# Seven block products for the second product of both feed-forward blocks, all joins on ScalarE, sums and scores in PSUM, byte masks, three transposition buffers and a new written order

## The chip, the core and the metric

One NeuronCore of a Trainium2 chip runs the whole program. The engines are TensorE (PE, matrix products into PSUM; its weight loads are listed as PEld), VectorE (DVE), ScalarE (ACT), GpSimd (POOL) and SyncE (SP), whose queue issues nearly all DMA transfers. All data are float32. The time is the device time of one launch in microseconds (us); the kernel before took 3119.91, 3129.46 and 3135.92 us in three runs, so the median is 3129.46 us.

## What is computed

64 independent graphs of 256 nodes with 256 features go through two layers. Cut to what matters:

```python
# layer 0
h = gat(x, adj, W1, a1); h = gat(h, adj, W2, a2)      # e = leaky_relu(Wh1 + Wh2^T), masked where adj <= 0,
h = layernorm(x + h, g_ln1, b_ln1)                    # softmax over axis 1, att @ Wh
x = layernorm(h + relu(h @ w_ff1 + b_ff1) @ w_ff2 + b_ff2, g_ln2, b_ln2)
# layer 1, 8 heads of width 32
p = softmax(q @ k^T / sqrt(32))
out = sum over r of (p * (adj == r)) @ v_r            # r = 0..3
x = layernorm(x + out @ Wo + bo, g1, beta1)
x = layernorm(x + gelu(x @ W1 + b1) @ W2 + b2, g2, beta2)
```

The inputs hold only 0 and 1 in `adj`, which the fast path (`binary`) uses: `v_0` is applied to all of `p`, and `v_1 - v_0` to `p * adj`. A slow path (`general`) stands behind a test of the maxima of `adj` and is not entered with these inputs.

## The kernel before

**Stages.** A graph passes through many small pieces of work, each a Python closure under a name. The letter is the stage: `L` loads, `G` the two attention steps of layer 0 and norm A, `F` the first feed-forward block with norm B and the projections, `A` the eight attention heads, `T` the output projection, norm C, the second feed-forward block, norm D and the store. `S` pieces prepare weights once. Nodes and features are both cut into two halves of 128, so a 256x256 matrix is 2x2 blocks.

**Order.** The order of all instructions on PE, DVE, ACT, POOL and SP is written out by hand in three lists (L43 to L158) and kept as written: `START`, then `PERIOD` once for each of 59 periods, then `END`. An entry such as `T.fa/5` means piece `T.fa` of the graph five behind the newest. So six graphs are in flight at once, and one graph is finished in each period. Every engine works its own share of the list in order; an instruction whose input is late holds all behind it on its engine.

**Seven products.** `seven_products` (L597) multiplies two matrices of 2x2 blocks with seven block products and sums of blocks instead of eight. Its pieces are `a` to `e` (the products, into three PSUM banks X, Y, Z), `k1` to `k4` (a first result taken out of a bank) and `p1` to `p3` (a bank added to a result, L637). It serves the first product of both feed-forward blocks (`h`, PE L661), the values of the heads (`v`, PE L848) and the second product of the block in `T` only (`f`, PE L702, with its sums `T.u0` to `T.u3` on POOL at L584 into the tile `H`). The second product of the block in `F` is plain: `F.f0` and `F.f1` (L682 to L689), 8 products each of 128x128 by 128x256 into the bank `ff_a`. Each float32 product shows as two instructions in the trace.

**Turning by DMA.** `turned` (L461) transposes a tile in three steps: `dt` (SP L469) a transposing DMA into `pairs`, `dm` (SP L477) two copies by DMA into `halves`, and a join (L484), a copy that interleaves 16-bit halves. `pairs` and `halves` have two tiles each. The joins of the eight heads are `A.mg00` to `A.mg13`, where the first digit is the group of four heads; head 0 of both groups is joined on POOL, the other six on ACT. The joins into columns (`F.cA`, `F.cB`, `T.cC`) are on ACT.

**Norms.** `layernorm` (L493): `ln` adds the residual on DVE (L502) into the SBUF tile `acc` and takes the moments (L507 to L510), `rs` takes the root on POOL (L514), `nm` writes the normed rows on DVE (L519).

**Scores of layer 0.** For steps A and B: `G.e` puts target scores in a PSUM bank (L763), `G.lr` adds source scores on ACT into the SBUF tile `s` (L771), `G.ad` does the leaky ReLU (L776), the mask (L777, with the byte tile `away`) and the maximum (L779) on DVE in place, `G.ex` the exponential on ACT (L784), `G.rz` scales the rows on DVE (L794), and `G.gA0`, `G.gA1`, `G.gB` are products (L800).

**Masks of the heads.** `A.pm` (L922) multiplies a joined head by the int32 tile `adj` on DVE. `adj` has four tiles, since a graph's adjacency lives from its load to its last head.

Of the kernel before, what the change touches and what calls it, by code (L numbers as in the profile page):

```python
# [25 lines left out]
F32 = mybir.dt.float32  # L26
U8 = mybir.dt.uint8
# [7 lines left out]
P = 128  # L35
# [8 lines left out]
G.nmA/1 A.mx13/3 A.rz12/3 F.raB/4 F.sB/3 T.hk3/5 A.mx11/3 A.rz10/3 L.xT/0 T.hp3/5 A.vp2/4 A.dm02/4  # L44
A.pm03/4 G.wh0/0 A.mg02/4 T.hd/5 A.ex13/3 T.hp2/5 G.wh1/0 A.ex11/3 A.sp12/3 A.dm00/4 G.wc0/0
A.sp10/3 G.wc1/0 A.ve/4 A.pm01/4 F.dtA/1 A.mg00/4 F.dmA/1 F.f1/2 A.pm02/4 G.eA/0 A.pm00/4 T.rbC/5
F.rbB/4 A.vk4/4 T.he/5 T.ge0/5 A.rz11/3 A.pm11/4 A.rz13/3 A.dt10/3 F.lnB/2 A.sc0/3 A.o0/4 T.ge1/5
A.mx00/3 G.lrA/0 F.cA/1 T.hk4/5 A.o1/4 T.ge2/5 A.sp11/3 A.sp13/3 A.mx02/3 A.dt12/3 F.ha/1 A.oc0/4
T.ge3/5 L.adj/0 A.oc1/4 F.sA/1 A.ex00/3 F.hb/1 A.mx03/3 G.away/0 A.dm10/3 A.dm12/3 F.rsB/2 F.hk1/1
F.hk2/1 T.wo/4 A.mx01/3 G.adA/0 A.mg10/3 T.u0/5 F.hp1/1 T.lnC/4 F.hc/1 T.u1/5 A.mg12/3 A.dt13/3  # L50
G.exA/0 F.raA/1 A.dt11/3 F.nmB/2 A.ex03/3 A.dm13/3 G.rzA/0 T.fa/5 F.hk3/1 A.ex02/3 T.rsC/4 T.fb/5
F.hd/1 T.nmC/4 G.gA0/0 T.u3/5 T.fk1/5 T.fk2/5 A.rz03/3 A.ex01/3 T.u2/5 F.hp2/1 L.x/0 F.hp3/1
A.mg13/3 A.sp03/3 G.gA1/0 A.pm12/3 G.wd0/0 G.wd1/0 A.dm11/3 A.rz01/3 T.fc/5 A.va/3 A.vb/3 F.dtB/2
T.fk3/5 A.mg11/3 F.rbA/1 A.sp01/3 F.r0/1 A.pm13/3 T.dtC/4 A.rz02/3 A.vk1/3 G.eB/0 T.fd/5 F.dmB/2
T.fp1/5 A.vk2/3 G.lrB/0 T.fp2/5 F.cB/2 F.he/1 A.vc/3 T.dmC/4 T.fe/5 A.rz00/3 F.r1/1 G.adB/0
A.dt03/3 T.cC/4 A.dt01/3 F.q/2 A.vk3/3 G.exB/0 F.hk4/1 A.vp3/3 T.fp3/5 F.qe0/2 F.k/2 A.sp02/3
T.fk4/5 F.r2/1 T.ha/4 F.qe1/2 A.dm03/3 F.ke0/2 T.hk1/4 T.lnD/5 G.rzB/0 T.nmD/5 A.sp00/3 T.sC/4
G.gB/0 A.vp1/3 T.hb/4 A.dm01/3 T.rsD/5 A.dt02/3 T.raC/4 F.ke1/2 T.rbD/5 T.hp1/4 A.sc1/2 T.out/5
A.dt00/3 G.lnA/0 A.mg03/3 T.hk2/4 F.r3/1 A.mg01/3 A.mx12/2 A.mx10/2 A.vd/3 G.rsA/0 T.hc/4 A.pm10/3
F.f0/1 A.ex12/2 A.ex10/2  # L60
# [5 lines left out]
G.away:0 L.adj:2 S.lw:0 S.v0:0 L.adj:1 G.wh0:0 G.wh1:0 G.wc0:0 G.wc1:0 G.eA:0 G.lrA:0 G.adA:0  # L66
S.f0:0 G.exA:0 G.rzA:0 G.gA0:0 G.gA1:0 G.wd0:0 G.wd1:0 S.f1:0 G.eB:0 G.lrB:0 S.f2:0 L.xT:1 G.wh1:1
G.adB:0 G.wh0:1 L.xT:2 G.exB:0 G.rzB:0 G.wc0:1 G.wc1:1 G.gB:0 G.wh0:2 G.eA:1 G.away:1 G.lrA:1
G.lnA:0 G.rsA:0 G.nmA:0 G.adA:1 F.dtA:0 F.raA:0 G.exA:1 S.p2:0 S.v1:0 G.wh1:2 S.q0:0 G.wc0:2
G.rzA:1 G.wc1:2 G.gA0:1 G.gA1:1 L.xT:3 G.eA:2 G.wd0:1 F.dmA:0 S.v2:0 S.q1:0 G.wd1:1 G.eB:1 F.cA:0  # L70
G.lrB:1 F.sA:0 G.adB:1 G.lrA:2 L.x:1 F.ha:0 S.lr:0 F.hk1:0 F.hb:0 G.away:2 G.adA:2 F.hk2:0 F.hc:0
F.hk3:0 F.hp3:0 F.hd:0 F.hp2:0 G.exB:1 F.he:0 F.r0:0 F.hp1:0 G.wh1:3 G.rzB:1 S.j1:0 G.gB:1 G.lnA:1
F.r1:0 F.hk4:0 F.r2:0 F.r3:0 G.wh0:3 F.f0:0 G.wc0:3 G.exA:2 L.adj:3 G.rsA:1 G.nmA:1 G.rzA:2 F.f1:0
G.gA0:2 F.rbA:0 G.gA1:2 F.lnB:0 G.wd0:2 L.x:2 L.xT:4 G.wc1:3 S.v3:0 G.wh1:4 G.wd1:2 F.rsB:0
F.dtA:1 F.dmA:1 G.eA:3 G.eB:2 G.lrB:2 F.cA:1 F.nmB:0 G.wh0:4 G.adB:2 G.lrA:3 F.ha:1 F.sA:1 G.exB:2
F.hb:1 F.dtB:0 F.hk1:1 F.raB:0 G.rzB:2 G.away:3 F.dmB:0 F.hk2:1 G.gB:2 G.lnA:2 G.wc0:4 F.cB:0
F.hc:1 F.k:0 G.adA:3 G.rsA:2 G.wc1:4 G.nmA:2 F.hk3:1 F.ke0:0 F.q:0 F.ke1:0 F.hp3:1 F.hd:1 F.qe0:0
L.x:3 F.hp1:1 F.hp2:1 F.qe1:0 F.r0:1 A.sc1:0 F.raA:1 A.mx13:0 F.he:1 A.mx10:0 F.r1:1 A.ex13:0
F.dtA:2 F.hk4:1 F.rbB:0 F.raA:2 F.r2:1 A.sc0:0 F.r3:1 A.rz13:0 A.mx12:0 A.mx00:0 A.sp13:0 F.dmA:2
G.exA:3 A.ex10:0 A.ex12:0 A.mx01:0 A.ex01:0 A.dt13:0 A.rz10:0 G.rzA:3 A.rz12:0 F.cA:2 F.sB:0  # L80
F.f0:1 F.f1:1 G.gA0:3 A.sp10:0 F.rbA:1 A.dm13:0 A.mx02:0 A.ex02:0 A.mg13:0 A.dt10:0 A.rz01:0
A.ex00:0 G.wd0:3 G.gA1:3 A.sp12:0 F.lnB:1 A.dt12:0 A.va:0 A.vb:0 A.mx11:0 G.wd1:3 A.sp01:0 F.rsB:1
A.vk1:0 G.eB:3 A.dm10:0 A.dm12:0 A.mg10:0 F.nmB:1 G.lrB:3 F.dtB:1 A.ex11:0 A.mg12:0 A.mx03:0
S.l0:0 F.ha:2 F.hk1:2 A.rz00:0 A.dt01:0 G.adB:3 A.pm10:0 A.rz11:0 F.sA:2 A.vk2:0 F.dmB:1 A.rz02:0
F.hb:2 F.hk2:2 A.dm01:0 A.vc:0 F.hc:2 A.ex03:0 S.l1:0 A.vk3:0 A.pm13:0 A.vd:0 F.cB:1 A.sp11:0
A.rz03:0 F.k:1 G.exB:3 A.vp1:0 F.hk3:2 A.mg01:0 A.sp02:0 F.ke0:1 F.hp1:2 G.rzB:3 F.hp3:2 F.q:1
A.dt11:0 F.rbA:2 A.vp2:0 F.ke1:1 F.hd:2 A.ve:0 F.qe0:1 F.qe1:1 A.dt02:0 A.dm11:0 A.sp00:0 F.hp2:2
G.gB:3 A.pm12:0 A.dm02:0 A.vk4:0 A.sp03:0 G.lnA:3 S.l2:0 A.mg11:0 F.he:2 F.r0:2 A.sc1:1 G.rsA:3
A.mx11:1 F.hk4:2 A.mg02:0 A.mx12:1 A.vp3:0 A.ex11:1 A.sc0:1 F.r1:2 A.dt03:0 A.rz11:1 A.mx13:1
# [97 lines left out]
def binary(ctx: ExitStack, tc: tile.TileContext, t, most, out: bass.AP):  # L187
# [1125 lines left out]
```

## Time and profile before

The profiled execution took 3121.47 us, of which its span is 3119.7 us; the median of the three timed runs is 8.0 us above it. The granted clock of TensorE was 0.992 of full speed over the span.

| what | us | share of the span | per graph (by 64) |
|---|---|---|---|
| TensorE busy | 3007.0 | 96% | 47.0 |
| VectorE busy | 2747.0 | 88% | 42.9 |
| ScalarE busy | 2548.7 | 82% | 39.8 |
| GpSimd busy | 2290.2 | 73% | 35.8 |
| DMA engines, mean of 16 | | 68% on SP's queue | |

A busy TensorE is one with a product in its pipeline, so its share says that it is seldom empty, not that it runs at its peak. For the slope one reads the distance from one group of products to the next. VectorE, ScalarE and GpSimd are given as the time in which an instruction ran.

### The profile page before, as it was taken

What the parts mean: (1) busy time and instruction counts of PE and PEld (TensorE: products, weight loads), DVE (VectorE), ACT (ScalarE), POOL (GpSimd) and SP (SyncE); (2) the same over time, 40 slices, a digit from 0 to 9 for tenths busy, and PEclk for the clock granted to TensorE, in tenths of its full rate; (3) what the DMA queues carried; (4) which work ended last, traced back from release to release, by engine and by line L of the source; (5) the groups of instructions that cost most, each with busy time, mean ns of one, the idle gap of its engine ahead of it and who ended that gap; (6) DMA issues with size and microseconds to landing.
All of it is one profiled execution on the core that took longest, in us unless ns stands there. A gap on an engine that the chain in (4) does not pass through costs nothing.

```text
span 3119.7 us, 68789 instructions
## 1 busy us (share of the span) xinstructions
PE 3007.0 (96%) x23270; PEld 2629.7 (84%) x23270; DVE 2747.0 (88%) x5744; ACT 2548.7 (82%) x5822; POOL 2290.2 (73%) x3057
## 2 busy tenths in 40 slices
PE   6899999999999999999999999999999999999986
PEld 5788888888888888888898888888888888888876
DVE  5689999899998899898999899999999999889965
ACT  2688888888888888888888888888888888878874
POOL 4568777777777777777777777777777777777765
PEclk9999999999999999999999999999999999999998
DMA  5577766677676777776676666677677776767663
GB/s 156 108 145 149 149 149 143 146 155 143 149 151 137 142 146 151 148 152 138 155 150 144 148 142 145 150 152 147 147 153 145 149 149 143 146 138 151 149 133 73
DMA packets 1023941, 449.41 MB, mean 144 GB/s; under 512 B 771008, under 2 KB 1021888, under 8 KB 1023584
## 3 DMA queue, kind: packets, MB, share of 16 engines
q1 hardware_dynamic: 1022320, 442.70, 67.9%
q8 instruction: 188, 3.08, 0.5%
q0 software_dynamic: 976, 1.72, 0.4%
q14 instruction: 169, 1.38, 0.2%
q10 hardware_dynamic: 288, 0.52, 0.1%
HBM read 58.87 MB, written 16.78 MB: 24 GB/s over the span
## 4 chain that ended last, share of the span: by engine, by line
PE 68%; DVE 12%; DMA 8%; issue 3%; ACT 3%; POOL 1%; SPq 1%; DVEq 0%; ACTq 0%; POOLq 0%
PE ff_a L686 11%; PE hX_c L661 6%; PE o L930 5%; PE fX_c L702 5%; PE hX_a L661 4%; PE sc L880 3%; PE q L835 3%; PE hY_c L661 3%; PE k L835 3%; PE gat_b L800 3%; PE vX L848 3%; PE wh L747 3%; DVE pm L922 2%; PE wo L949 2%; DMA adj<-in_adjT 2%
## 5 line engine op out<-in xcount | busy, mean ns | idle before, releaser
L484 ACT COPY pm<-halves_p 128x1024 uint16<-128x1024 uint16 x384 | 522.4, 1360 | 137.8 <-DMA halves_p<-pairs_p 135.7
L922 DVE TENSOR_TENSOR pm<-pm,adj 128x512 f32<-128x512 f32 x512 | 565.6, 1123 | 19.3 <-POOL pm L484 12.2
L686 PE MATMUL ff_a<-w_L_gnn_w_ff,hid_a 128*128 128x256 f32 x2048 | 463.0, 379 | 0.1
L686 PEld LDWEIGHTS ff_a<-w_L_gnn_w_ff,hid_a 128*128 128x128 f32 x2048 | 384.0, 190 | 50.4 <-ACT hid_a L678 0.8
L484 POOL COPY pm<-halves_p 128x1024 uint16<-128x1024 uint16 x128 | 180.2, 1408 | 157.5 <-DMA halves_p<-pairs_p 140.4
L930 PE MATMUL o<-pm,v 128*32 128x256 f32 x4096 | 235.3, 381 | 5.5 <-POOL p L907 2.4
L678 ACT ACTIVATE hid_a<-hid_a,col_L_gnn_b_ff 128x256 f32<-128x256 f32 x512 | 230.1, 500 | 3.3 <-DVE hid_a L637 3.2
L678 ACT ACTIVATE hid_c<-hid_c,col_L_gnn_b 128x256 f32<-128x256 f32 x512 | 224.4, 498 | 5.1 <-DVE hid_c L637 2.4
L930 PEld LDWEIGHTS o<-pm,v 128*32 128x32 f32 x4096 | 126.2, 110 | 104.6 <-issue 15.9
L702 PE MATMUL fX_c<-f_L_gnn_W,hid_c 128*128 128x128 f32 x1536 | 207.2, 278 | 7.3 <-ACT hid_c L678 5.1
L514 POOL TENSOR_TENSOR rstd_a<-var_a,neghalf 128x2 f32<-128x2 f32 x64 | 45.0, 702 | 222.5 <-DVE var_a L510 222.5
L702 PEld LDWEIGHTS fX_c<-f_L_gnn_W,hid_c 128*128 128x128 f32 x1536 | 192.8, 192 | 13.2 <-ACT hid_c L678 5.8
L661 PEld LDWEIGHTS hX_a<-cols_a,f_L_gnn_w_ff 128*128 128x128 f32 x1024 | 126.9, 195 | 33.1 <-ACT hid_c L678 22.2
L880 PE MATMUL sc<-kT,qT 32*128 32x256 f32 x2048 | 149.6, 400 | 3.3 <-ACT p L894 2.8
L584 POOL TENSOR_TENSOR S_c<-cols_c 128x128 f32<-128x128 f32 x128 | 58.3, 455 | 128.4 <-ACT cols_c L484 128.4
L800 PE MATMUL gat_a<-whz_A,s_A 128*128 128x258 f32 x512 | 134.9, 400 | 18.2 <-DVE whz_A L794 15.4
L661 PE MATMUL hX_a<-cols_a,f_L_gnn_w_ff 128*128 128x128 f32 x1024 | 144.6, 285 | 6.4 <-ACT cols_a L484 5.0
L747 PE MATMUL wh<-wx,xT 128*128 128x260 f32 x512 | 136.0, 390 | 12.5 <-DVE wx L372 10.1
L661 PEld LDWEIGHTS hX_c<-S_c,f_L_gnn_W 128*128 128x128 f32 x1024 | 134.0, 191 | 8.5 <-ACT hid_c L672 1.3
L702 PE MATMUL fY_c<-f_L_gnn_W,H_c 128*128 128x128 f32 x1024 | 137.3, 278 | 3.8 <-POOL H_c L584 3.8
L661 PE MATMUL hX_c<-cols_c,f_L_gnn_W 128*128 128x128 f32 x1024 | 135.8, 276 | 2.7 <-ACT cols_c L484 2.7
L661 PE MATMUL hX_a<-S_a,f_L_gnn_w_ff 128*128 128x128 f32 x1024 | 136.9, 277 | 0.0
(2760 smaller groups left out, 9808.9 us busy)
## 6 DMA issues: line engine op xcount, KB each, us to landing
halves_p<-pairs_p SPq DMA_DIRECT2D x1024, 128.0 KB, 3.3
xT<-in_xT SPq DMA_DIRECT2D x64, 256.0 KB, 3.4
adj<-in_adjT SPq DMA_DIRECT2D x64, 256.0 KB, 3.5
x<-in_x SPq DMA_DIRECT2D x64, 256.0 KB, 3.5
halves_y_a<-pairs_y_a SPq DMA_DIRECT2D x128, 128.0 KB, 3.0
halves_y_y<-pairs_y_y SPq DMA_DIRECT2D x128, 128.0 KB, 3.5
halves_y_c<-pairs_y_c SPq DMA_DIRECT2D x128, 128.0 KB, 3.2
out<-res_d SPq DMA_DIRECT2D x64, 256.0 KB, 2.6
```

The costliest lines, as they stand in the source:

```text
L484: copy(into().bitcast(U16).rearrange("p (n s) -> p s n", s=2), t["halves"].rearrange("p s k q -> p s (k q)"),)
L661: nc.tensor.matmul(ps[:, f * P : (f + 1) * P], weights()[0][:, factor, f * P : (f + 1) * P], left, start=start and f == 0, stop=f == FC // ...
L678: nc.scalar.activation(tiles["hid"][:, f, :], tiles["hid"][:, f, :], func, bias=b1[:, f : f + 1])
L686: nc.tensor.matmul(tiles["ff"][:, i, :], tiles["hid"][:, f, nodes(i)], weights()[2][:, f, :], start=(f == 0), stop=(f == FC - 1),)
L702: nc.tensor.matmul(ps, left[:, f, :], weights()[2][:, factor, f * P : (f + 1) * P], start=start and f == 0, stop=f == FC // 2 - 1, skip_gr ...
L747: nc.tensor.matmul(t["whp", j], tiles["xT"][:, c, nodes(j)], wx[:, c, :], start=(c == 0), stop=(c == KC - 1),)
L800: nc.tensor.matmul(ps, t["s"][:, j, nodes(i)], t["whz"][:, j, :width], start=(j == 0), stop=(j == NT - 1),)
L835: nc.tensor.matmul(t[key + "p"][:, o, :], w[:, c, nodes(o)], tiles["cols"][:, c, :], start=(c == 0), stop=(c == KC - 1),)
L848: nc.tensor.matmul(ps, left, wv[:, factor, :], start=start, stop=True, skip_group_check=True)
L880: nc.tensor.matmul(t["sc", g, hh][:, i, :], qkv["q"][hd, g, nodes(i)], qkv["k"][hd, g, :], start=True, stop=True,)
L922: nc.vector.tensor_tensor(pm[:, 1, :], pm[:, 0, :], tiles["adj"], ALU.mult)
L930: nc.tensor.matmul(ps[hh * DH : (hh + 1) * DH, :], qkv["v"][:, j, d0 : d0 + DH], t["pm", (g, hh)][:, r, j * N : (j + 1) * N], start=(r == ...
```

## The change

Seven edits, and new lists `START`, `PERIOD` and `END` (208 entries in the period where there were 194: sixteen pieces come and two go; all others are moved about).

1. The block in `F` uses the seven products for its second product too. `F.f0` and `F.f1` go; `F.fa` to `F.fe`, `F.fk1` to `F.fk4`, `F.fp1` to `F.fp3` and the sums `F.u0` to `F.u3` come. Its weights are loaded as four blocks and their three differences (piece `S.o2`, four subtractions on POOL).
2. All eight heads' joins are on ACT.
3. Norms A and C add the residual in the PSUM bank of the product; norm B takes the finished rows from the new pieces, which add the residual themselves.
4. The scores of layer 0 are held in their PSUM bank from the leaky ReLU to the exponential.
5. The heads are masked with the byte tile `away`; `away` has four tiles, `adj` one.
6. `pairs` and `halves` have three tiles each; `p` five for four, `pm` seven for eight, `s` and `whz` one for two.
7. The first weights: W1 on ACT's DMA queue, products with W1 ahead of those with W1W2, and their sums written where they are used.

```diff
-    joined = work.tile([P, 4, D], F32, tag="pm", name="joined", bufs=8)
+    joined = work.tile([P, 4, D], F32, tag="pm", name="joined", bufs=7)
...
-            adj = tiles["adj"] = io.tile([P, NT * N], I32, tag="adj", name=f"adj_{b}", bufs=4)
+            adj = tiles["adj"] = io.tile([P, NT * N], I32, tag="adj", name=f"adj_{b}", bufs=1)
...
-        for w, n in ((w1T, "L0_gnn_W1T"), (w2, "L0_gnn_W2"), (w1, "L0_gnn_W1")):
-            nc.sync.dma_start(out=w, in_=t[n].rearrange("(c p) n -> p c n", p=P))
+        for queue, w, n in (
+            (nc.sync, w1T, "L0_gnn_W1T"), (nc.scalar, w1, "L0_gnn_W1"), (nc.sync, w2, "L0_gnn_W2"),
+        ):
+            queue.dma_start(out=w, in_=t[n].rearrange("(c p) n -> p c n", p=P))
...
-        nc.vector.tensor_copy(wx[:, :, :D], ps)
-        for w, a, at in ((wx, a2, SRC2), (w1, a1, SRC1)):
+        for w, a, at in ((w1, a1, SRC1), (wx, a2, SRC2)):
+            if w is wx:
+                nc.vector.tensor_copy(wx[:, :, :D], ps)
             for c in range(KC):
...
+                for half in range(2):
+                    nc.vector.tensor_tensor(prod[:, half, :], a[:, 1 - half, :], w[:, c, :D], ALU.mult)
+                nc.vector.tensor_reduce(wx[:, c, at : at + 2], prod, AX.X, ALU.add)
...
-    ff0 = w1, column("L0_gnn_b_ff1"), weight("L0_gnn_w_ff2", FC)
+    w2, out_differences = out_factors("L0_gnn_w_ff2")
+    ff0 = w1, column("L0_gnn_b_ff1"), w2
...
-            t["pairs"] = work.tile([P, 2, 4, P], U16, tag="pairs", name=f"pairs_{name}", bufs=2)
+            t["pairs"] = work.tile([P, 2, 4, P], U16, tag="pairs", name=f"pairs_{name}", bufs=3)
...
-            t["halves"] = work.tile([P, 2, 4, P], U16, tag="halves", name=f"halves_{name}", bufs=2)
+            t["halves"] = work.tile([P, 2, 4, P], U16, tag="halves", name=f"halves_{name}", bufs=3)
...
-            acc, *terms = src()
-            if terms:
-                acc = work.tile([P, NT, D], F32, tag="acc", name=f"acc_{name}", bufs=2)
-                nc.vector.tensor_tensor(acc, *terms, ALU.add)
+            acc, *residual = src()
+            if residual:
+                nc.vector.tensor_tensor(acc, acc, *residual, ALU.add)
...
-            nc.vector.scalar_tensor_tensor(t["s"], t["s"], ALPHA, t["s"], ALU.mult, ALU.max)
-            nc.vector.scalar_tensor_tensor(t["s"], t["away"], NEG, t["s"], ALU.mult, ALU.add)
+            nc.vector.scalar_tensor_tensor(t["e"], t["s"], ALPHA, t["s"], ALU.mult, ALU.max)
+            away = tiles["away"].rearrange("p (t i) -> p t i", t=NT)
+            nc.vector.scalar_tensor_tensor(t["e"], away, NEG, t["e"], ALU.mult, ALU.add)
...
-                    t["s"][:, j, :], t["s"][:, j, :], AF.Exp,
+                    t["s"][:, j, :], t["e"][:, j, :], AF.Exp,
...
-            nc.vector.tensor_tensor(pm[:, 1, :], pm[:, 0, :], tiles["adj"], ALU.mult)
+            nc.vector.scalar_tensor_tensor(
+                pm[:, 1, :], tiles["away"], 0.0, pm[:, 0, :], ALU.is_equal, ALU.mult
+            )
...
-                    partial(both, h), "POOL" if hh in ((0,), (0,))[g] else "ACT",
+                    partial(both, h), "POOL" if hh in ((), ())[g] else "ACT",
...
-        feed_forward(do, "F", f"a{b}", a, lambda: ff0, "r", AF.Relu, seven=False)
-        y = layernorm(do, "F", "B", f"b{b}", lambda: (None, a["ff"], a["res"]))
+        feed_forward(do, "F", f"a{b}", a, lambda: ff0, "r", AF.Relu)
+        y = layernorm(do, "F", "B", f"b{b}", lambda: (a["ff"],))
```

## The prediction

> **What bounds the kernel now.** I read the engines' busy shares first, over the stretch from 300 to 2900 us in which only the period runs, then the chain of waits inside one period, then the rate at which finished graphs are stored, then who waited for whom.
>
> ```profile
> 300.00:2900.00 2600.00, 2563.18 (x20075) 2248.68 (x20074) 2375.54 (x4949) 2210.40 (x5049) 1957.62 (x2605) 1.00 0.71 147
> ...
> 1505.59 3.45 PE ff_a L686 x16
> ...
> 1521.21 0.89 PE fX_c L702 x8
> 1522.11 0.89 PE fZ_c L702 x8
> ...
> 229.37 0.58 SPq L992 DMA_DIRECT2D out<-res_d  x1
> ...
> 2943.48 0.58 SPq L992 DMA_DIRECT2D out<-res_d  x1
> ```
>
> The first row gives PE 98.6% of the stretch, DVE 91.4%, ACT 85.0%, POOL 75.3%, at full granted clock. The next three are steps of the chain of waits: nearly every piece of it in a period is PE, and its pieces follow each other without a gap. So the slope of PE can be read there: 8 products of 128x256 (16 instructions) take 3.45 us, 4 products of 128x128 take 0.89 us. The last two are the first and the 59th store: (2943.48 - 229.37) / 58 = 46.80 us for a period.
>
> Adding the chain's pieces of one graph: 21 groups of 128x128 at 0.892 (18.73), the plain second product 2 x 3.45 (6.90), heads 3.59, scores 2 x 1.075, four groups at 1.73 (q, k, wo, gat_b: 6.92), gat_a 1.75, wh 1.76, values 7 x 0.43, transposes 0.44: **45.25 us of PE work**, so 1.55 us of each period are stalls. PE sets the pace, but the stalls have other causes:
>
> ```profile
> DVE away L739 <- DMA adj<-in_adjT: 57.2, 41, 3.6
> ...
> ACT pm L484 <- DMA halves_p<-pairs_p: 108.3, 76, 5.2
> POOL pm L484 <- DMA halves_p<-pairs_p: 116.4, 58, 4.0
> ```
>
> These are sums of waits over the same 2600 us, with their number and the longest. In the slowest period (50.3 us, stores at 2755.84 and 2806.16) the chain passes through a load of `xT` of 5.92 us and one of `adj` of 5.74, each issued just before its use.
>
> **The seven products in F.** Removed on PE: 6.90 us per graph. Added: 28 products in seven groups, 7 x 0.892 = 6.24. Gain 0.66 us, times 64 graphs = **42.2 us**, all on the bounding engine. It is less than an eighth of 6.90 (0.86), because products of half the width run at 0.223 us each and not at half of 0.431. Added elsewhere: four sums on POOL as those of T (rows L584 for `H_c` and `hid_c`: 102.3 + 93.4 + 88.7 + 85.2 = 369.6 us, 5.78 per graph); seven small DVE steps like T's (rows L713 and L637 on `acc_c`: 123.2 us, 1.93 per graph), less the add of norm B (L502, 0.67): DVE +1.26. They hide beside PE as T's do; `F.fb` needs `F.u0` (1.6 us on POOL), and between the last ReLU and `F.fb` the new order has `wo` and `F.fa`, 3.5 us of PE work.
>
> **All joins on ACT.** POOL loses 2 x 1.41 = 2.8 us per graph, ACT gains 2 x 1.36 = 2.7. If nothing hid it, 2.7 us a period; what hides it is ACT's idle 15%, 7.0 us.
>
> **PSUM for sums and scores.** The trace has no DVE norm out of PSUM and no mask into it. Bounds for the norm's 128x256: the two-source rows of that size with a PSUM input, 0.41 us, and today's means, 0.70 (`y_a`) and 0.87 (`y_c`). For the scores' mask of 128x512: 0.69 (L502, a PSUM input) and today's 1.42 and 0.84. I take the lower values, because the long rows are waits and not work:
>
> ```profile
> L777 DVE SCALAR_TENSOR_TENSOR s_A<-away,s_A x55: 691/1647/1797, 342.7 to 2874.0; 128x512 f32<-128x512 uint8 x55
> ...
> L922 DVE TENSOR_TENSOR pm<-pm,adj x442: 660/938/1776, 306.9 to 2886.6; 128x512 f32<-128x512 f32 x148
> ```
>
> The three numbers are least, median and most in ns: the same instruction takes 0.69 or 1.65. The Trainium skill, "SBUF — State Buffer", section "Who interferes with whom", gives the reason: DVE and GpSimd share a port pair under an exclusive lock; a DVE instruction with two SBUF inputs, or in a two-port mode, is held by a GpSimd one that reads SBUF, and one with a single SBUF input is not. With one input in PSUM the norms A and C fall from 190.9 us (2.98 per graph) to 4 x 0.41 (-1.34), the scores' masks from 2.26 to 1.38 (-0.88). By rows without the rule both would stay: 0. Neither is on the chain. Adds and maxima cost the same from PSUM (0.685 at L887, 0.686 at L779). Holding banks longer could block PE; but counting banks along the written orders from each piece that takes one to the last that reads it, both orders need at most 8, and 5.8 on average before, 5.6 after, since `ff_a` no longer holds one from `F.f0` to norm B.
>
> **Masks by bytes.** Two SBUF inputs as before. Bounds per mask: floor 0.69 against 0.66, ceiling 1.80 against 1.78; for eight, from -3.3 us (all at the floor) to +5.5 (all at the ceiling). Nearest is no change; with POOL busier I add 0.2 us.
>
> A rule that speaks against the change: "GPSIMD Engine Reference", section "Engine selection", says elementwise adds belong on VectorE, GpSimd being about twice slower with two inputs. The rows agree on speed (1.44 against 0.67). By the rule the four sums would put 2.7 us on DVE: 42.9 + 1.26 - 1.34 - 0.88 + 0.2 + 2.7 = 44.8 of a 45 to 46 us period, which would make DVE the bound. On POOL DVE has **42.1**, POOL 35.8 - 2.8 + 5.8 = **38.8**, ACT 39.8 + 2.7 = **42.5**, PE **44.6**. The row decides for POOL.
>
> **Buffers and order.** Joins follow their copies sooner than a copy lands (3.3 us): PE work between the two in the written order is 2.4 us on average over the eight heads before, and 3.7 after. From `L.adj` to `G.away` it grows from 0.9 to 6.5 us, from `L.xT` to `G.wh0` from 0 to 0.9. Third tiles of `pairs` and `halves` loosen SP's queue, which waited 370.6 us for the `pairs` tile to be read. Two switches of ACT's table per period in both orders. Against this stand the two joins that ACT takes over with their waits. The bounds of the stalls: 0.3 us a period (-74 us over 59) to the rival below; I take -0.5 for the loads and copies and +0.3 for the fuller ACT, so -0.2 x 59 = **-12 us**.
>
> **Start.** The first `wh` runs at 22.04 us, after 6.5 us of small DVE steps on the first weights that begin at 16.50, behind a wait for `adj`. With those of W1 done earlier some 3 us of steps remain: 22.0 becomes 15.8 or, if `adj` holds them, 19.5. I take **-4**. The four weight differences on POOL (5.2 us by L258) lie in its idle time before 29 us.
>
> **Sum:** 3121.5 - 42.2 - 12 - 4 = 3063 us against the profiled execution's own time. The timed median is 8.0 above that one, so the forecast for the median is **3071**.
>
> **Rivals.**
> 1. *The order does better* (0.16): the loads' stalls go almost whole, 0.7 us are left: 3129.5 - 42 - 50 - 4 = 3033 (3000 to 3045).
> 2. *Half is lost* (0.13): ACT's fuller queue hands waits to PE, 0.3 us a period more than today: 3129.5 - 42 + 18 = 3105 (3095 to 3120).
> 3. *ACT becomes the bound* (0.10, slower): POOL's joins wait 116.4/110 = 1.06 us each for their copies, ACT's own 0.33. With eight joins ACT must fit 42.5 us, and breaks even with the old period if its idle time is at most 46.8 - 42.5 = 4.3 us; now it is 7.0. If it only falls to 5.5, the period is 48.0, +1.2 x 59 = +71: 3200. Against it: DVE today has 42.8 us of work in 46.8 and PE does not stop for it.
> 4. *The busy sums are right* (0.03, slower): by busy time T's second product costs 487 us (207.2 + 137.3 + 71.8 + 70.4), more than the plain 463.0. Then +24 us: 3153. Against it: the chain shows groups of 0.89 with no gap; busy time counts the filling of the pipeline twice where groups of other pieces lie between.
>
> **How the numbers follow.** The likeliest case (0.58) covers 3045 to 3095. About what can be told from no change is 0.5%, 3114 to 3145. Faster: the likeliest, the first rival and 0.10 of the second, 0.84; same: the second's rest, 0.03; slower: the third and fourth, 0.13. The range 3022 to 3122 leaves out the tail of the first rival (0.06) and the slower cases (0.13).
>
> **What would show it.** Right: stores 45.5 to 46.2 us apart; groups `fX_a`, `fY_a`, `fZ_a` at 0.89 in the chain; norms of a and c near 0.41 and the scores' masks near 0.7 with no long rows; the wait of `away` for `adj` gone; ACT at 91 to 94%. Wrong: ACT or POOL in the chain of every period, PE waiting for `cols` or for `hid_a` after `F.u`, joins waiting over 1 us each, or PE groups of `f` in F stretched beyond 0.9.

## The result, and the profile after

The changed kernel takes **3091.74 us** (median of four runs, 3088.8 to 3097.2); the kernel before, on the same chip, 3127.83 (3119.91 to 3135.92). The ratio is **0.9887, 95% interval 0.9857 to 0.9916**: faster by 1.1%. The forecast was 3071 within 3022 to 3122, so the direction and the range held, and the gain is 36 us where 57 were foreseen. The profiled execution took 3090.9 us, of which its span is 3089.0. One launch of the experiments, of the run with two joins on GpSimd, had a granted clock of 0.75 and took 3796.96 us; it is left out of that run's time.

Where the time went is read from the stores, as before the change. Two rows of the order of events on SP's queue (start in us, duration, queue, line, kind) give the first and the 59th store of the changed kernel, and a row of the windows view gives the engines' busy time between (length, PE, PE's weight loads, DVE, ACT, POOL, then granted clock, DMA share, GB/s):

```profile
222.91 0.41 SPq L991 DMA_DIRECT2D out<-res_d  x1
...
2895.47 0.41 SPq L991 DMA_DIRECT2D out<-res_d  x1
```

```profile
300.00:2900.00 2600.00, 2566.22 (x21750) 2285.23 (x21749) 2246.26 (x5361) 2358.37 (x5239) 2086.53 (x2768) 1.00 0.76 149
```

(2895.47 - 222.91) / 58 = 46.08 us a graph, where it was 46.80. PE is busy 98.7% (98.6% before), DVE fell to 86.4%, ACT rose to 90.7%, POOL to 80.3%. The span splits into three:

| part | before | after | difference |
|---|---|---|---|
| up to the first store | 229.4 | 222.9 | -6.5 |
| 58 intervals of stores | 2714.1 | 2672.6 | -41.5 |
| behind the 59th store | 176.2 | 193.5 | **+17.3** |

So the steady part gave nearly what was foreseen for it, and the last graphs took 17 us of it back.

The waits of TensorE changed their place. This is the view of who waited for whom between 300 and 2900 us (sum in us, number, longest), first of the kernel before, then of the changed one:

```profile
PE gat_a L800 <- DVE whz_A L794: 11.8, 23, 1.0
PE fX_c L702 <- DVE acc_c L713: 10.6, 32, 1.1
PE q L835 <- ACT cols_y L484: 6.9, 11, 1.1
PE fZ_c L702 <- DVE hid_a L637: 4.5, 5, 1.7
```

```profile
PE hX_c L668 <- ACT cols_c L491: 27.3, 34, 1.8
PE hX_c L668 <- ACT hid_c L679: 3.5, 8, 0.7
PE wh L741 <- DMA xT<-in_xT: 2.6, 7, 0.8
```

Four small waits at four places are gone. In their stead stands one that matters: `T.ha`, the first product of the T block, waits for its columns `cols_c`. The order of events in one period shows the chain behind it:

```profile
1538.40 1.97 PE L948 MATMUL wo<-w_L_gnn_Wo,oT 128*128 128x256 f32 x8
...
1538.89 1.27 POOL L591 TENSOR_TENSOR H_a<-hid_a 128x512 f32<-128x512 f32 x1 [1.16 <-ACT hid_a L685]
...
1540.23 1.28 POOL L591 TENSOR_TENSOR H_a<-H_a,hid_a 128x512 f32<-128x512 f32 x1
...
1541.59 1.27 POOL L591 TENSOR_TENSOR H_a<-hid_a,H_a 128x512 f32<-128x512 f32 x1
...
1542.98 0.70 POOL L521 TENSOR_TENSOR rstd_c<-var_c,neghalf 128x2 f32<-128x2 f32 x1
...
1543.71 1.00 DVE L526 TENSOR_SCALAR y_c<-wo,mv_c,rstd_c 128x256 f32<-128x256 f32 x2
...
1545.42 1.65 SPq L476 DMA_TRANSPOSE pairs_y_c<-y_c  x1
...
1549.16 1.20 SPq L484 DMA_DIRECT2D halves_y_c<-pairs_y_c  x2
...
1552.99 1.33 ACT L491 COPY cols_c<-halves_y_c 128x1024 uint16<-128x1024 uint16 x1 [1.62 <-DMA halves_y_c<-pairs_y_c]
...
1554.38 1.16 PE L668 MATMUL hX_c<-cols_c,f_L_gnn_W 128*128 128x128 f32 x8 [0.52 <-ACT cols_c L491]
```

From the end of `wo` at 1540.4 to `hX_c` at 1554.4 pass 14.0 us: norm C on DVE, its root `rstd_c` on POOL (queued behind three of the new sums of F, `H_a`), two DMAs of some 3.8 us each, the join on ACT. TensorE's work written between `T.wo` and `T.ha` is about 13.4 us, and the seven products of F lie in it. The brackets show the idle time before an instruction: ACT stood 1.62 us before the join and PE 0.52 before the product.

### The profile page after: what moved, and what is told of

Same layout as the page of the kernel before. It is cut to its first block, busy times and chain, and to the rows that moved or that the text cites. A ratio compares the mean times of both kernels' runs of the same rounds, so it can differ in the third digit from the quotient of the medians.

```text
span 3089.0 us, 72126 instructions
## 1 busy us (share of the span) xinstructions
PE 2974.5 (96%) x24806; PEld 2634.4 (85%) x24806; DVE 2572.8 (83%) x6124; ACT 2677.4 (87%) x5950; POOL 2404.5 (78%) x3189
## 4 chain that ended last, share of the span: by engine, by line
PE 73%; DMA 10%; ACT 7%; POOL 4%; DVE 3%; issue 2%; SPq 1%; ACTq 0%; POOLq 0%; DVEq 0%
PE o L929 7%; PE hX_c L668 7%; PE fX_c L700 7%; PE hX_a L668 6%; DMA halves_y_c<-pairs_y_c 4%; PE sc L877 4%; PE fX_a L700 4%; PE wh L741 4%; PE fY_c L700 3%; PE k L832 3%; PE gat_b L797 3%; PE hY_c L668 3%; PE hY_a L668 3%; PE q L832 3%; PE wo L948 3%; PE fY_a L700 3%
## 5 line engine op out<-in xcount | busy, mean ns | idle before, releaser
L491 ACT COPY pm<-halves_p 128x1024 uint16<-128x1024 uint16 x512 | 680.8, 1369 | 49.1 <-DMA halves_p<-pairs_p 48.9
L919 DVE SCALAR_TENSOR_TENSOR pm<-away,pm 128x512 f32<-128x512 uint8 x512 | 439.9, 888 | 29.6 <-ACT pm L491 29.4
L521 POOL TENSOR_TENSOR rstd_a<-var_a,neghalf 128x2 f32<-128x2 f32 x64 | 67.2, 1049 | 257.8 <-DVE var_a L517 253.6
L700 PEld LDWEIGHTS fX_a<-f_L_gnn_w_ff,hid_a 128*128 128x128 f32 x1536 | 200.4, 191 | 18.4 <-DVE acc_a L644 3.7
L700 PE MATMUL fX_a<-f_L_gnn_w_ff,hid_a 128*128 128x128 f32 x1536 | 204.9, 276 | 3.9 <-ACT hid_a L685 1.3
L668 PEld LDWEIGHTS hX_c<-cols_c,f_L_gnn_W 128*128 128x128 f32 x1024 | 132.7, 194 | 65.0 <-ACT cols_c L491 60.3
L668 PE MATMUL hX_c<-cols_c,f_L_gnn_W 128*128 128x128 f32 x1024 | 142.6, 283 | 43.7 <-ACT cols_c L491 43.5
L561 POOL TENSOR_TENSOR res_b<-y_b,row_L_gnn_g_ln 128x256 f32<-128x256 f32 x128 | 97.2, 780 | 105.5 <-DMA out<-res_d 76.1
L491 ACT COPY cols_c<-halves_y_c 128x1024 uint16<-128x1024 uint16 x64 | 85.6, 1338 | 107.6 <-DMA halves_y_c<-pairs_y_c 107.6
L591 POOL TENSOR_TENSOR S_c<-cols_c 128x128 f32<-128x128 f32 x128 | 74.3, 580 | 97.0 <-ACT cols_c L491 71.7
L591 POOL TENSOR_TENSOR H_a<-hid_a 128x512 f32<-128x512 f32 x64 | 81.4, 1272 | 78.8 <-ACT hid_a L685 78.8
```

Source lines behind the costliest of these rows:

```text
L491: copy(into().bitcast(U16).rearrange("p (n s) -> p s n", s=2), t["halves"].rearrange("p s k q -> p s (k q)"),)
L561: nc.gpsimd.tensor_tensor(tiles["res"][:, i, :].rearrange("p (k c d) -> p c k d", k=KC, c=2), tiles["y"][:, :, :, i, :], rows[g].rearrange ...
L591: engine.tensor_tensor(to[i], one, other, op)
L668: nc.tensor.matmul(ps[:, f * P : (f + 1) * P], weights()[0][:, factor, f * P : (f + 1) * P], left, start=start and f == 0, stop=f == FC // ...
L700: nc.tensor.matmul(ps, left[:, f, :], weights()[2][:, factor, f * P : (f + 1) * P], start=start and f == 0, stop=f == FC // 2 - 1, skip_gr ...
L919: nc.vector.scalar_tensor_tensor(pm[:, 1, :], tiles["away"], 0.0, pm[:, 0, :], ALU.is_equal, ALU.mult)
```

## The experiments

In every run below the steady part is given as the interval of the stores, (59th - first) / 58, and the end as the time from the 59th store to the end of the span. The kernel before, measured beside each group of runs, had medians of 3129.8 to 3132.7 us, so medians of different groups can differ by 3 us for that reason alone. The changed kernel was measured a second time:

> The changed kernel itself, once more, as the measure for the runs beside it. Both theories expect 3092 us within 5, and the spread of its runs says what a difference between the others has to exceed.

3094.28 us (3091.73 to 3096.35), ratio 0.988 (0.9863 to 0.9896); stores 46.14 apart, end 193.8. Between the two profiles of one kernel the interval differs by 0.06 us and the end by 0.3; smaller differences say nothing. Waits below are sums from 300 to 2850 us. Costs for a graph below are against the mean of the two, 46.11.

### The seven products of F

```diff
+            do["F.fb"], do["F.fd"] = partial(plain, 0), partial(plain, 1)   # 8 products of 128x256 each
+            # F.fa, fc, fe, F.fk*, F.fp*, F.u*: nothing
-        y = layernorm(do, "F", "B", f"b{b}", lambda: (a["ff"],))
+        y = layernorm(do, "F", "B", f"b{b}", lambda: (a["ffp"], a["res"]))
```

> The changed kernel with only the second product of block F plain again (16 products of 128x256 in place of 7x4 of half the width; no sums F.u, no merges, the norm adds the residual). PE has 0.66 us more of work for a graph, GpSimd 5.1 us less, VectorE about 1.4 us less. Theory (TensorE's work sets the steady part): the stores are 46.7 to 46.9 us apart, and the time is 3125 to 3140. Rival (relief or load of the other engines sets it, and the gain came from joins, PSUM sums, masks and order): the interval stays within 0.2 of 46.1, and the time is 3080 to 3100.

3111.59 us (3108.65 to 3117.38), ratio 0.9939 (0.9925 to 0.9953); stores 46.36 apart, end 194.7. **Between the two expectations.** Taking the seven products out costs 0.25 us a graph (and 3107.6 - 3091.8 = 15.8 us of span), though it adds 0.66 of TensorE work. The waits say where the other 0.41 went:

```profile
PE wo L963 <- DVE acc_c L644: 3.6, 15, 0.3
PE hX_c L668 <- ACT hid_c L679: 3.5, 7, 0.6
PE hX_c L668 <- ACT cols_c L491: 1.9, 6, 0.5
```

Without the seven products the wait for `cols_c` is 1.9 us in all in place of 26.6 in the changed kernel's second profile (55 graphs): 0.45 a graph less. So the seven products pay 0.66 and give some 0.4 back to this one wait. Two things could make them do that: the F products between `T.wo` and `T.ha` became shorter (cover), or their sums on GpSimd hold `rstd_c` up. Two runs were made to separate them.

```diff
-                      *(f"fp{c}" for c in "123"), *(f"u{c}" for c in "0123")):
+                      *(f"fp{c}" for c in "123")):     # plain product, sums kept
```

> The run with the plain second product of F, with the four sums F.u still made on GpSimd and read by nothing. TensorE's work is that of the plain product, GpSimd's that of the changed kernel. Theory A (cover): as in the run without the sums, stores 46.3 to 46.5 us apart, hX_c waits for cols_c under 5 us in all. Theory B (GpSimd's sums delay norm C): hX_c waits for cols_c 20 us or more in all, and the stores are 46.7 us apart or more.

3110.23 us (3108.39 to 3113.62), ratio 0.9932 (0.9913 to 0.9951); stores 46.33 apart, end 195.5. (The fourth sum overwrites a quarter of the hidden values that the plain product still reads, so the output differs; the work is the same.) The interval is that of theory A; the wait for `cols_c`, 9.8 us where it was 1.9, lies above A's 5 and below B's 20. So both theories have a part in the wait: with the wide cover the sums add 0.15 us a graph to it (9.8 against 1.9), and with the sums the narrow cover adds 0.30 (26.6 against 9.8).

```diff
-            engine = nc.gpsimd if ('POOL', 'POOL')[stage == "T"] == "POOL" else nc.vector
+            engine = nc.gpsimd if ('DVE', 'POOL')[stage == "T"] == "POOL" else nc.vector
```

> The changed kernel with the four sums F.u of block F on VectorE in place of GpSimd, in the same order: GpSimd has 5.1 us a graph less, VectorE 4 x 0.6 to 1.1 us more. It tells apart two causes of the wait of hX_c for cols_c. Theory A (cover: the narrower second product left 0.66 us less of TensorE work between T.wo and T.ha, the chain of norm C, its turn and its join is as long as before): the wait stays at about 0.5 us a graph and the stores stay 46.0 to 46.3 us apart, or more if VectorE is late with the norm. Theory B (the sums on GpSimd delay rstd_c, which is queued behind them): the wait goes, and the stores are 45.5 to 45.8 us apart.

3178.27 us (3177.16 to 3181.05), ratio 1.0155 (1.0135 to 1.0174), slower than the kernel before; stores 47.55 apart. The sums take 0.69 us each on VectorE and 1.27 on GpSimd, and still VectorE is the wrong place:

```profile
PE hX_c L668 <- ACT cols_c L491: 22.8, 23, 1.4
PE fX_a L700 <- DVE H_a L591: 20.3, 54, 0.4
PE fX_a L700 <- DVE acc_a L644: 17.7, 54, 0.3
```

Two new waits come in every period: TensorE waits for the sums and for the merges queued behind them. VectorE was busy only 88% of the stretch. It did not become the bound by its load but by its queue. The old wait stays, but this doesn't decide for theory A: with the sums in its queue VectorE is itself late with norm C.

The traces settle it. These are means over the graphs from 300 to 2850 us, worked out from the start and end of each instruction, in us from the end of `wo`: when `rstd_c` starts, when `cols_c` is joined, how long TensorE is busy before `T.ha`, and when `T.ha` starts.

| run | `rstd_c` starts | `cols_c` joined | TensorE busy | `T.ha` starts |
|---|---|---|---|---|
| plain, no sums (e2) | 2.33 | 13.47 | 14.02 | 14.06 |
| plain, sums kept (e6) | 2.61 | 13.74 | 14.04 | 14.23 |
| changed kernel | 2.61 | 13.76 | 13.44 | 13.93 |
| sums on VectorE (e5) | 2.93 | 14.93 | 13.94 | 15.07 |
| kernel before | 3.44 | 16.80 | 17.75 | 18.40 |

The sums on GpSimd make the chain 0.28 us longer, and the seven products make the cover 0.60 us shorter. By these figures each alone would leave the chain about as long as the cover or shorter (a short cover without any sums was not run); together they put the columns 0.32 us behind TensorE on average. The last row adds that the tight fit is also the new order's: before, the chain was 3 us longer, but TensorE had 4.3 us more of work to do beside it.

### The joins on ScalarE

```diff
-                    partial(both, h), "POOL" if hh in ((), ())[g] else "ACT",
+                    partial(both, h), "POOL" if hh in ((0,), (0,))[g] else "ACT",
```

> The changed kernel with two of a graph's eight joins of the attention (heads 00 and 10) on GpSimd again, as before: ScalarE has 2.7 us a graph less, GpSimd about 2.5 to 4.9 us more, the order is the same. Theory (TensorE sets the steady part; ScalarE at 91% is no bound): the time moves by less than 10 us, 3082 to 3102. Rival (ScalarE's queue is the limit, the wait for cols_c shows it): ScalarE gets free earlier, the stall at hX_c shrinks by half or more, and the time falls to 3060 to 3080. If GpSimd, at 43 us of a 46 us period, holds its products back, the time grows to 3110 or more.

3174.94 us (median of four, 3166.43 to 3180.43), ratio 1.0143 (1.0124 to 1.0162); stores 47.23 apart, end 197.8. Of the three expectations only the last holds: 1.1 us a graph **slower**. A join is no dearer on GpSimd (1.34 us against 1.37), and ScalarE is down to 84% of the stretch. What it costs is a place in the queue. The waits of GpSimd and of TensorE in this run:

```profile
POOL pm L491 <- DMA halves_p<-pairs_p: 79.1, 46, 3.5
```

```profile
PE hX_c L668 <- ACT cols_c L491: 32.6, 32, 3.0
PE hX_c L668 <- ACT hid_c L679: 31.0, 43, 0.9
PE vX L845 <- DVE v L644: 10.4, 25, 0.9
```

GpSimd stands before a join for its DMA, and by the written order norms' roots and sums are queued behind it; TensorE waits at the products these lead to. Is it the sums of F that leave GpSimd no room?

```diff
# both edits together: the plain second product of F, and the two joins on GpSimd
```

> The plain second product of F, and two joins of the attention a graph on GpSimd again: both undone, all the rest of the change kept. GpSimd then has 5.1 us of sums less and 2.7 us of joins more than in the changed kernel. If the joins had to leave GpSimd only because of the sums, this costs little against the plain product alone: stores 46.3 to 46.7 us apart, 3105 to 3130 us. If a join on GpSimd is late by itself (it waits for its DMA at the head of a queue that holds norms and sums), it costs as much as in the run with the sums, 1.1 us a graph: 47.2 to 47.5 us, 3165 to 3185.

3189.15 us (3182.58 to 3195.5), ratio 1.0179 (1.0156 to 1.0202); stores 47.73 apart. Even without the sums the two joins on GpSimd cost 1.37 us a graph against the plain product alone (46.36), more than the 1.1 with the sums and than the 47.2 to 47.5 that were expected. So in this order moving the joins is worth more than the seven products (1.1 against 0.25 us a graph), and the two are no package. It also shows what the new order is written for: the old product and the old joins take 47.73 us in it, with the change's other edits, and took 46.80 in their own.

### Scores in PSUM, masks by bytes

```diff
-            nc.vector.scalar_tensor_tensor(t["e"], away, NEG, t["e"], ALU.mult, ALU.add)
+            nc.vector.scalar_tensor_tensor(t["s"], away, NEG, t["s"], ALU.mult, ALU.add)
# likewise the leaky ReLU before it, the maximum and the exponential behind it
```

> The changed kernel with the GAT's scores masked and exponentiated in their SBUF tile again in place of PSUM; all else the same. Prediction's step: masks of the scores 0.69 us from PSUM, against 0.84 and 1.42 in SBUF before. If what made them long was the collision with GpSimd, they are 0.7 where GpSimd pauses and up to 1.4 where it doesn't. Theory (not on TensorE's path): stores 46.0 to 46.3 us apart, 3088 to 3100. Rival (the PSUM scores are what made the wait of gat_a go): the waits of gat_a are back with 10 us or more in all, and the time is 3105 or more.

3120.41 us (3117.38 to 3124.38), ratio 0.9971 (0.996 to 0.9982); stores 46.51 apart, end 193.1. The wait of `gat_a` did not come back, and yet this costs 0.40 us a graph, as much as the rival asked for. The groups of VectorE (busy us, mean ns of one), first of the changed kernel, then of this run:

```profile
L774 DVE SCALAR_TENSOR_TENSOR e_A<-away,e_A 128x512 f32<-128x512 uint8 x64 | 44.5, 696 | 2.2
L774 DVE SCALAR_TENSOR_TENSOR e_B<-away,e_B 128x512 f32<-128x512 uint8 x64 | 44.5, 695 | 2.2
```

```profile
L774 DVE SCALAR_TENSOR_TENSOR s_A<-away,s_A 128x512 f32<-128x512 uint8 x64 | 108.8, 1700 | 2.2
...
L774 DVE SCALAR_TENSOR_TENSOR s_B<-away,s_B 128x512 f32<-128x512 uint8 x64 | 53.7, 839 | 2.2
```

The mask of step A is 1.0 us longer out of SBUF, in nearly every period (its median is 1753 ns), and in the new order VectorE reaches norm C (`T.lnC`) right behind it. Counted as in the table above, `rstd_c` starts 3.44 us after `wo` in place of 2.61, and `cols_c` is joined at 14.33 in place of 13.76. The wait for `cols_c` grew (30.9 us, 39 times, and for its weight loads 51.0 against 43.7). These waits account for only part of the 0.40 us. Still, a saving that looked as if it lay beside TensorE's work lies on the chain.

```diff
-                pm[:, 1, :], tiles["away"], 0.0, pm[:, 0, :], ALU.is_equal, ALU.mult
+                pm[:, 1, :], wk.rearrange("p c n -> p (c n)").bitcast(I32), 0.0, pm[:, 0, :],
+                ALU.is_equal, ALU.mult,
```

> The changed kernel with the heads' masks reading four bytes an element (a resident weight tile of the same shape in place of the byte mask; the masking by relation is left out, the amount of work is the same). Prediction's step: byte masks against four-byte masks are worth between 0 and 0.25 us each, 2.0 us of VectorE a graph, all of it beside TensorE's work. Theory (TensorE and the chain of norm C set the period): masks of 0.95 to 1.15 us, the stores 46.0 to 46.4 us apart. Rival (the masks end the wait for pm, and the gain of the change came from them): 46.6 us or more, 3120 or more.

3097.47 us (3090.78 to 3099.76), ratio 0.9886 (0.9865 to 0.9908); stores 46.21 apart. The tile view of `pm` (least, median and most, ns), changed kernel and this run:

```profile
L919 DVE SCALAR_TENSOR_TENSOR pm<-away,pm x512: 672/686/1801, 136.8 to 3041.8; 128x512 f32<-128x512 uint8 x171
```

```profile
L919 DVE SCALAR_TENSOR_TENSOR pm<-w_L_gnn_Wk,pm x512: 669/686/1809, 136.7 to 3051.2; 128x512 f32<-128x512 int32 x171
```

One byte or four: the same. The masks nevertheless got shorter: their mean was 1123 ns before and is 888 now, 1.9 us a graph for the eight (the median went from 936 to 686), and e8 rules the bytes out as the cause. The start times in the traces show the one that is left. A mask that starts while GpSimd is in one of the residual's scalings (`res_a`, `res_b`, `res_c`) ends some 0.55 us after that instruction, in both kernels, and one with no GpSimd instruction beside it takes 0.68. Of the 512 masks 228 started inside such a scaling before, and 125 do now; 30 started inside a join on GpSimd, and now none does. With the joins back on GpSimd (e3) the mean is 876, so it is the new order that keeps them apart. The bytes themselves free space for the third tiles.

### The wait that is left

If the wait for `cols_c` were all, more work before `T.ha` would take it away. TensorE's queue in the steady order, cut to the place:

```diff
- ... A.vd T.ha A.ve T.hb F.hb T.hc F.hc T.hd ...
+ ... A.vd A.ve F.hb T.ha T.hb T.hc F.hc T.hd ...
```

> The changed kernel with the first product of the T block (T.ha, with its copy T.hk1) two places later in the steady order, behind A.ve and F.hb: 1.3 us more of TensorE work lie between its columns' turn and the product. Theory (what is left of the steady stall is this one wait, hX_c for cols_c, 0.5 to 0.6 us a graph, and nothing else is late): the stores are 45.5 to 45.8 us apart and the time is 3064 to 3080. Rival (the wait only moves to the next product that hangs on the same chain): the interval stays at 46.0 to 46.2 and the time within 6 us of the changed kernel's.

3121.55 us (3113.72 to 3124.59), ratio 0.9963 (0.9949 to 0.9976); stores 46.56 apart: 27 us slower. The wait is gone, and another is there:

```profile
PE vX L845 <- DVE v L644: 28.2, 55, 0.5
PE wh L741 <- DMA xT<-in_xT: 2.0, 3, 0.9
PE hX_c L668 <- ACT hid_c L679: 2.0, 5, 0.6
```

`A.ve` adds to a bank that VectorE must first have read after `A.vd`, and `T.ha` had covered that. The move was mine and badly placed; it shows that the pieces around `T.ha` cover each other, but doesn't say what the wait is worth.

The other way is to shorten the chain itself, and touch no queue but VectorE's:

```diff
-        c = layernorm(do, "T", "C", f"c{b}", lambda: (heads["wo"], y["res"]))
+        c = layernorm(do, "T", "C", f"c{b}", lambda: (heads["wo"],))
```

> The changed kernel with norm C's addition of the residual left out (one VectorE instruction of 0.69 us a graph; the output lacks that term). It shortens the chain from T.wo over norm C, the turn and the join to T.ha by 0.65 us and touches no other engine. Theory (what is left of the steady waits is this one chain): the wait of hX_c for cols_c falls from 27 us to under 8, the stores are 45.5 to 45.8 us apart, and the time is 3060 to 3080. Rival (the join waits for its place on ScalarE or for the DMA queue anyway, or the wait moves on): the interval stays at 46.0 to 46.2 and the time at 3085 to 3098.

3098.61 us (3094.46 to 3107.47), ratio 0.9903 (0.988 to 0.9927); stores 46.22 apart, the wait for `cols_c` 30.7 us. **My theory fell:** 0.69 us taken out of the chain gains nothing. The figures lie at the edge of the rival's, but the reason is none that it names. It is a row that should not have changed, the variance of norm C, an instruction on two elements a partition (the run with the plain product and no sums, e2; then the changed kernel; then this run):

```profile
L517 DVE TENSOR_SCALAR var_c<-mv_c 128x2 f32<-128x2 f32 x64 | 11.3, 177 | 2.2
```

```profile
L517 DVE TENSOR_SCALAR var_c<-mv_c 128x2 f32<-128x2 f32 x64 | 27.1, 424 | 2.2
```

```profile
L517 DVE TENSOR_SCALAR var_c<-mv_c 128x2 f32<-128x2 f32 x64 | 71.3, 1114 | 2.2
```

The instruction by itself takes 0.17 us. The whole 0.69 us reappears in it here. The order of events of this run shows what it waits for:

```profile
1546.20 1.27 POOL L591 TENSOR_TENSOR H_a<-hid_a,H_a 128x512 f32<-128x512 f32 x1
...
1546.32 1.19 DVE L517 TENSOR_SCALAR var_c<-mv_c 128x2 f32<-128x2 f32 x1
...
1547.58 0.70 POOL L521 TENSOR_TENSOR rstd_c<-var_c,neghalf 128x2 f32<-128x2 f32 x1
```

`var_c` begins 0.12 us after GpSimd's third sum and ends with it (1547.51 and 1547.47). The changed kernel is held too, only for less long: `var_c` begins at 1542.44 beside a sum that ends at 1542.86, and ends at 1542.89. On average the third sum ends 2.50 us after `wo` in both runs, and `rstd_c` starts at 2.61 in both; by itself `var_c` would end at 2.26 in the changed kernel and at 1.51 here. Either way `rstd_c` cannot start before the third sum is through, since it is queued behind it. So where `T.ha` waits, the chain begins earlier than I had drawn it: at the ReLUs of F on ScalarE (POOL idles 1.16 us for `hid_a` above), goes over three sums, and only then through `rstd_c`, the two DMAs and the join. Of norm C on VectorE and the sums on GpSimd the later one counts at `rstd_c`, and in the changed kernel that is the sums, by 0.24 us: shortening norm C gains nothing, and making it 1.1 us later (e11) delays `rstd_c` by 0.83. Whether `T.rsC` ahead of the third sum would shorten it was not tried.

### The end, and other orders

```diff
# END: the same 577 entries, in another order; START and PERIOD as they are
```

> The changed kernel with the same pieces in another order in the list of the end alone (the last graphs); steady order and start untouched. In the runs so far the stretch behind the 59th store took 192 to 198 us whatever was in it (plain second product of F, joins on GpSimd, sums on VectorE), against 176 in the kernel before. Theory (the 17 us that the end lost lie in the order of its list, not in its work): the stretch takes 178 to 188 us, the interval of the stores stays at 46.1, and the time is 3077 to 3088. Rival (the end costs what its longer chain of sums, joins and turns costs, or the lower clock): 190 us or more, 3090 to 3098.

3088.46 us (3083.64 to 3095.73), ratio 0.9872 (0.9853 to 0.9891); end 188.0, stores 46.14. The end is 5.8 us shorter, at the edge of what the theory asked for. The median is the lowest of all runs, but only 3.3 us below the changed kernel's first and 5.8 below its second, and the intervals of the ratios overlap. In the end's own stretch it settles a third of the 17 us. The windows behind the 59th store, of the kernel before, of the changed one and of this run:

```profile
2943.48:3003.48 60.00, 58.30 (x507) 50.24 (x505) 42.84 (x96) 49.27 (x109) 46.44 (x64) 1.00 0.67 135
3003.48:3063.48 60.00, 43.87 (x310) 36.08 (x303) 36.18 (x83) 40.25 (x88) 38.74 (x55) 0.89 0.65 138
3063.48:3119.70 56.22, 39.08 (x322) 33.94 (x321) 30.28 (x70) 17.60 (x32) 27.94 (x29) 0.92 0.20 49
```

```profile
2895.47:2955.47 60.00, 56.61 (x486) 49.80 (x485) 43.14 (x97) 48.79 (x101) 41.97 (x57) 0.97 0.67 124
2955.47:3015.47 60.00, 47.05 (x362) 37.30 (x361) 36.83 (x90) 41.46 (x93) 35.82 (x51) 0.89 0.57 111
3015.47:3089.00 73.53, 50.00 (x364) 44.50 (x363) 29.99 (x80) 30.41 (x53) 35.41 (x44) 0.83 0.32 69
```

```profile
2899.51:2959.51 60.00, 56.65 (x478) 49.10 (x480) 40.63 (x96) 49.15 (x101) 42.45 (x58) 1.00 0.61 119
2959.51:3019.51 60.00, 50.36 (x398) 39.21 (x391) 36.11 (x95) 45.78 (x102) 40.10 (x58) 0.94 0.72 132
3019.51:3087.50 67.99, 48.27 (x338) 40.80 (x336) 31.98 (x78) 25.37 (x44) 30.88 (x36) 0.83 0.34 60
```

In the changed kernel TensorE is busy 153.7 us in place of 141.3 and idle 39.9 in place of 35.0. Of the 12.4 us of busy time some 4.6 are work: counted along the written lists, `END` now holds 122.2 us of products where it held 117.6. The rest comes with a lower granted clock, 0.83 in the last stretch where it was 0.92. The other order of e9 takes 7.2 us of idle time away (32.7 are left, less than before) and none of the busy time, 155.3. So what is left of the loss lies in TensorE's busy time. But e9 has a clock of 1.00 and 0.94 in its first two stretches and isn't busy for less, so the clock alone doesn't explain it. How much of the 17 us is the clock, and whether the order brings it about, stays open.

```diff
# END as in e9. PERIOD: the same 208 entries, moved by a few places within the queues, e.g. on GpSimd
- ... T.raC F.sA T.rbC F.rsB T.rsD T.sC ...
+ ... F.sA T.rsD F.rsB T.raC T.sC T.rbC ...
```

> The same new list of the end, and a steady order with many small moves within the engines' queues, chosen so that short delays do less harm; no work differs. Theory (0.6 us a graph of waits is left in the steady part, which moves within the queues can partly win): stores 45.8 to 46.1 us apart, 3060 to 3085. Rival (moves only carry the wait to another product, as the later T.ha did): 46.1 to 46.6, 3080 to 3115.

3230.3 us (3228.15 to 3239.02), ratio 1.0335 (1.0316 to 1.0354); stores 48.58 apart, end 184.9. Worse than anything else, with the same work:

```profile
PE hX_c L668 <- ACT cols_c L491: 88.2, 53, 3.0
```

```profile
L526 DVE TENSOR_SCALAR y_b<-acc_a,mv_b,rstd_b 128x256 f32<-128x256 f32 x128 | 49.4, 428 | 95.0 <-POOL res_c L561 91.9 <-POOL rstd_b L521 3.1
```

Norm B (`y_b`) stands 1.4 us a graph on VectorE (91.9 over 64) until GpSimd has read norm C's rows for `res_c`, which is `T.raC`, now three places later on GpSimd; and the wait for `cols_c` trebles. Many entries moved, so no single one is shown to be the cause. But moves within the queues, with no work changed, cost 2.5 us a graph, ten times what the seven products gain here: the order is no detail of this change.

## Why the prediction was right, and where not

The forecast for the profiled execution was 3063 us, 58.2 below before; it is 30.6 below. Point by point:

- **The seven products, -0.66 us a graph.** The work went as counted, and undoing it costs only 0.25. The step failed in taking TensorE's work for time "all on the bounding engine". The products of F are also the cover of norm C's chain, and their sums on GpSimd lengthen that chain, so 0.41 of the 0.66 came back as a wait (runs e2, e6). Of the text's signs against it, "PE waiting for `cols`" came true; POOL is in the chain of waits in 16 of 56 periods (worked out from the changed kernel's trace), not in every one.
- **Buffers and order, -0.2 us a graph.** With the plain product in the new order the stalls, counted as in the prediction, are 46.36 - 45.25 = 1.1 us where they were 1.55: -0.44, against "-0.5 for the loads and copies". The "+0.3 for the fuller ACT" is +0.41, and not from ACT: its size came near by luck. The sum, some -0.05 in place of -0.2, is what the steady part fell short of: -41.5 us where 0.86 x 58 = 49.9 were foreseen. Two things in this step were mis-read. The 1.55 us were called stalls, but the first row that the prediction shows has TensorE idle for only 36.8 of 2600 us, 0.66 a graph; it is 0.60 in the changed kernel and 0.2 in e2. The other 0.9 us shows as idle time in none of the three, and what it is no run tells. And the four waits of TensorE that went were for VectorE and for one join; whether late loads and copies stood behind them is not shown. The waits that the step named did go: `away` no longer waits for `adj`, and SP's queue waits 2.2 us for `halves_p` where it waited 326.6 (300 to 2900 us); but no run undoes the order or the third tiles alone, so what gave the -0.44 stays open.
- **All joins on ACT.** Costed as a burden that ACT's idle time hides. ACT did hide it (90.7% busy, forecast 91 to 94), and the two joins' waits of GpSimd for their copies, 116.4 us, are gone, while ScalarE's fell from 108.3 to 42.3. Only the join of `cols_c` waits over 1 us each time (80.3 us, 57 times). But the edit is more than a hidden burden: it is a relief of GpSimd's queue, without which this order is 1.1 us a graph slower (e3, e7). "ACT becomes the bound", 3200 us, did not come: the text's own ground against it held.
- **Sums on GpSimd, not VectorE.** Rightly decided by the row. The Trainium skill's "GPSIMD Engine Reference", section "Engine selection", would put such sums on VectorE. There they are indeed about twice as fast, 0.69 us against 1.27, and yet the kernel takes 84 us more (3178.27 against 3094.28). The reason given, 44.8 us of VectorE work as the bound, was not it: VectorE was busy 88%, and what cost was the sums' place in its queue. On GpSimd a sum took 1.27, not 1.44, for F.
- **PSUM.** Scores' masks 0.696, forecast 0.69, with no long rows: right, and "neither is on the chain" was wrong, since step A's mask stands before norm C (e11: 0.40 us a graph). Norms A and C 0.54 us, forecast 0.41: mis-sized. 0.41 was the row of a two-source instruction. Norm B shows what the source does: out of SBUF `y_b` takes 0.42 in the changed kernel, and out of PSUM 0.54 in e2. So a source in PSUM costs 0.11 more here, and it is steadier than the 0.70 and 0.87 of before.
- **Masks by bytes, +0.2 us.** -1.9 us of VectorE, from fewer starts inside GpSimd's scalings and not from the bytes (e8). What the shorter masks are worth on TensorE's path was not measured.
- **Start, -4.** -6.5 us at the first store; but the first `wh` gained only 1.2 (22.04 to 20.85): the product W1W2 that it needs began at 9.60 before and now begins at 14.58, when its last weight has landed. The rest is spread over the first graphs, and no run separates it.
- **The end, nothing.** The missing term: +17.3 us, where what the sum left for the last graphs, 58.2 - 49.9 - 4, was -4.3. That is 21.6 us of the 27.6 by which the forecast missed. The steady part is 8.4 of it, and the start gave 2.5 back.

## What to carry to other kernels

TensorE at 98.7% does not make its work the price: the products between a producer and the late consumer of its turned result are cover, and shortening them pays only until that chain shows. To learn what a piece is worth in a hand-ordered kernel, take it out of the final order, since what looked like a side of this change (joins, scores in PSUM) was worth more there than its centre. And cost the start and the end as stages of their own, with their own order and their own clock.

## What the runs showed of the hardware

- A VectorE instruction on 2 elements a partition took 177 ns on average where no sum ran on GpSimd beside it (e2), 424 where a GpSimd sum of 128x512 was near its end, and 1114 when such a sum had begun just before it; it ended with the sum. The Trainium skill, "SBUF — State Buffer", section "Who interferes with whom", says that a VectorE `tensor_scalar` in a two-port mode is blocked for the whole of a GpSimd instruction that came first; the row agrees with the blocking, down to an instruction with almost no data, though no run shows in which mode it ran.
- The same section's other half, that one SBUF input outside these modes goes free, shows in the masks of the scores: 1700 and 839 ns with both inputs in SBUF, 696 and 695 with one in PSUM.
- A 128x512 mask with both inputs in SBUF took 0.68 us alone; when it started inside a GpSimd multiplication of two SBUF tiles (`res`), it ended some 0.55 us after that one did, in the kernel before (228 masks) and in the changed one (125).
- A join of 128x1024 16-bit elements takes 1.34 us on GpSimd and 1.37 on ScalarE; choosing the engine by duration would have told nothing of the 81 us between them (e3).
